# Earlier row writes beside the routing, and a fixed order for a slot's row numbers, in a four-layer mixture-of-experts kernel

## The chip, the cores and the metric

The kernel runs on one core of one Trainium2 chip, as one launch. The metric is the time of an execution on the device in microseconds (us), and the number that counts is the median over several runs. Inside the core, five engines take instructions from queues of their own and work through them in order: TensorE (PE) multiplies matrices, VectorE (DVE) and ScalarE (ACT) do elementwise work, GpSimd (POOL) and SyncE (SP) here mainly issue transfers. [...]

## The reference, cut to what matters

Four layers act on 2048 tokens of 256 channels. Each adds to the tokens the output of an expert network whose input is conditioned first:

```python
x = x + _L0_ffn_ref(_L0_cond_ref(x, cond_1024, ...), ...)
x = x + _L1_ffn_ref(_L1_cond_ref(x, cond_1024, ...), ...)
x = x + _L2_ffn_ref(_L2_cond_ref(x, cond_1024, ...), ...)
x = x + _L3_ffn_ref(_L3_cond_ref(x, cond_1024, ...), ...)
return x
```

Three of these steps have the shape that the change touches: a shared feed-forward network over all tokens, and eight routed experts of which each token uses two. `_L2_cond_ref` and `_L3_cond_ref` are

```python
shared = silu(xf @ w1) * (xf @ w3) @ w2
s = sigmoid(concat([xf, tf]) @ router_W)
_, topk_idx = top_k(s + router_bias, 2)
gates = s_sel / (denom + 1e-09)
h = gelu(einsum('nc,ech->enh', xf, W1e)); y = einsum('enh,ehc->enc', h, W2e)
out = (shared + einsum('ne,enc->nc', combine, y)) / (N_SHARED + 2)
```

and `_L2_ffn_ref` is the same with gated experts of 1024 hidden channels. Layer 2's conditioning has 1024 hidden channels in its shared part, layer 3's has 512. All numbers are 32-bit floats.

## The kernel before

**Tiling.** Tokens lie in SBUF twice: by channel (`XT`, `HT`) as input of matrix products, and by token in 16 tiles of 128 (`Xt`, `Ht`). Routed experts aren't computed densely. Each token's row is written to the DRAM buffer `xbuf` at a place sorted by expert, two places per token. A slot is then 128 such rows, all of one expert; 39 slots hold the 4096 rows with their padding. A slot's outputs go to `tbuf` by token, and the two rows of a token are summed later with their gates.

**The order of a step** (`_cond_moe` from L1493 for layer 2's and layer 3's conditioning, `_layer2_ffn` from L1596 for layer 2's main part; the trace names them l2c, l3c and l2f):

1. The shared part for three of the four token blocks (`_shared`, L1202). For each 128 hidden channels it makes two products `spg` and `spu` (L1215), a silu `ssg` on ACT (L1220), a product `sa` on DVE (L1222) and the second matrix product `spo` (L1225). After each it calls a hook. In l2c and l2f there are 8 such steps in a block, 24 in all; in l3c 4 in a block, 12 in all.
2. Into these steps the class `Lead` (L298) puts the routing. It cuts a generator `routing` in two parts: scores and ranks first, then, in the second part, row numbers, gates and the list of row writes (`lead.sends`, made by `Rows.paced`). `Lead(k, routing, at, per)` runs the parts at the hooks that `at` names: hooks 2 and 4 in l2c and l2f, 1 and 3 in l3c. At each later hook from `late` + 1 on it issues `per` row writes: two in l2c and l2f, four in l3c. There are 32 row writes, one for each of 16 token tiles and two choices.
3. A row write (`Rows.scatter`, L277) is an indirect transfer that POOL issues. When it comes from a hook it carries a real wait on that hook's `sa` product.
4. The slots. `Slots.rows` loads the slot's 128 rows into `xs` (L293, issued by SP; it waits for all 32 row writes), PE turns them (`ps_cm`, L350), DVE copies them to `xsT` (L1369). From two extra columns of `xs` DVE makes each row's target in `tbuf`: `sn` (L1373), 1 for a row that isn't of the slot's expert, and `sdst` (L1375). In the conditioning stages the slot's products are `cph` (L1394) with a gelu `ch` on ACT (L1397), `cpo` (L1400), and a copy `ys` on DVE (L1402). POOL writes `ys` to `tbuf` at `sdst` (L277 again).
5. The fourth token block of the shared part, into whose steps the sums by token are put, and then the next step or, behind l3c, the last expert layer.

**What sets the order.** The program is written as one sequence. A scheduler orders each engine's queue before the launch, by its own estimate of what is ready when; on the chip the order is fixed. `_behind(k, inst, ref)` (L1195) is an order for this scheduler alone: `inst` is put behind `ref` on its engine, with no semaphore. Tiles come from pools with a fixed number of buffers: `xs` has 4, `xsT` 3, `sn` 3, `sdst` 5, `ys` 4. An instruction that writes a tile waits until the readers of the buffer's former content are done; for `sdst` the reader is the row write to `tbuf`, for `xs` they are PE's turn and DVE's `sn` and `sdst`. Weights of a slot's expert (`ring`, L1351) are loaded by SP into four sets in turn.

Of the kernel before, what the change touches and what calls it, by code (L numbers as in the profile page):

```python
# [14 lines left out]
ALU = mybir.AluOpType  # L15
# [5 lines left out]
D = 256  # L21
# [19 lines left out]
class Ring:  # L41


    def __init__(self, t, n):
        self.t, self.n, self.i, self.held = t, n, 0, set()
# [215 lines left out]
class Rows:  # L261
# [12 lines left out]
    def scatter(self, rows, idx, ref=None, **end):  # L274

        k = self.k
        i = k.nc.gpsimd.indirect_dma_start(out=self.ap, out_offset=bass.IndirectOffsetOnAxis(ap=idx, axis=0),  # L277
                                           in_=rows, in_offset=None, **end)
        group = "%s%d" % (self.ap.tensor.name, self.n)
        k.tc.declare_no_dep(i.ins, group=group, reason="rows of their own")  # L280
        k.tc.add_to_no_dep_group(group, i.ins)
        _after(k, i, self.old)
        if ref is not None:
            _after(k, i, [ref.ins.name])
        self.new.append(i.ins.name)

    def paced(self, rows, idxs):

        todo = [(rows[:, t, :], idx[:, t:t + 1]) for t in range(NT) for idx in idxs]
        return [lambda ref=None, a=a: self.scatter(*a, ref) for a in todo]  # L290
# [7 lines left out]
class Lead:  # L298
# [2 lines left out]

    def __init__(self, k, routing, at, per):
        self.k, self.at, self.per = k, at, per
        self.n, self.sends, self.made, self.late = 0, [], None, max(at) + 1 if max(at) else 0
        self.parts = routing(self)
        while 0 in self.at:
            self.part()
# [5 lines left out]
    def hook(self, f, mul, mm):  # L313
        self.n += 1
        if self.n in self.at:
            self.part()
        elif self.n > self.late:
            for _ in range(min(self.per, len(self.sends))):
                self.sends.pop(0)(mul)
# [26 lines left out]
def _channel_major(k, psum, rows):  # L346

    ps = psum.tile([P, 2, P], F32, name="ps_cm", tag="t", bufs=2)
    for c in range(2):
        k.nc.tensor.transpose(ps[:, c, :], rows[:, c * P:(c + 1) * P], k.ident)  # L350
    return ps
# [19 lines left out]
def _layer0(k):  # L371
# [6 lines left out]
    with ExitStack() as ctx:  # L378
# [59 lines left out]
        def shared(tb, hook=None):  # L438
            po = _shared(k, pool, psum, HT, tb, *shw, hook)
            for i in range(2):  # L440
                t = tb * 4 + i * 2
                nc.vector.tensor_tensor(Xt[:, t:t + 2, :], po[i], Xt[:, t:t + 2, :], ALU.add)
# [752 lines left out]
def _behind(k, inst, ref):  # L1195

    k.tc.add_manual_dep(inst.ins, ref.ins.name,
                        mybir.DependencyInfo(mybir.DependencyClass.NoSync,
                                             mybir.DependencyReason.SCHED_ONLY))


def _shared(k, pool, psum, X, tb, W1, W3, W2, nf, hook=None, mid=None):  # L1202

    nc = k.nc
    cols = slice(tb * TB, (tb + 1) * TB)
    po = [psum.tile([P, 2, D], F32, name="spo%d" % i, tag="o", bufs=2) for i in range(2)]
    mul = None
    for f in range(nf):  # L1210
        pg = psum.tile([P, TB], F32, name="spg", tag="mm")
        pu = psum.tile([P, TB], F32, name="spu", tag="mm")
        for ps, W in ((pg, W1), (pu, W3)):
            for c in range(2):
                mm = nc.tensor.matmul(ps, W[:, c, f * P:(f + 1) * P], X[:, c, cols],  # L1215
                                      start=c == 0, stop=c == 1)
        if mid:
            mid(f, mul, mm)
        sg = pool.tile([P, TB], F32, name="ssg", tag="sg")
        nc.scalar.activation(sg, pg, AF.Silu)  # L1220
        a = pool.tile([P, TB], F32, name="sa")
        mul = nc.vector.tensor_mul(a, sg, pu)  # L1222
        for g in range(4):

            mm = nc.tensor.matmul(po[g // 2][:, g % 2, :], a[:, g * P:(g + 1) * P], W2[:, f, :],  # L1225
                                  start=f == 0 and g % 2 == 0, stop=f == nf - 1,
                                  skip_group_check=True)
        if hook:
            hook(f, mul, mm)
    return po  # L1230
# [124 lines left out]
class Slots:  # L1355
# [7 lines left out]
    def rows(self, i):  # L1363

        k, nc, pool = self.k, self.k.nc, self.pool
        xs = pool.tile([P, DR], F32, name="xs", bufs=4)
        k.x.load(xs, k.xbuf[i * P:(i + 1) * P, :])
        xT = pool.tile([P, 2, P], F32, name="xsT", bufs=3)
        nc.vector.tensor_copy(xT, _channel_major(k, self.psum, xs))  # L1369
        if self.of is not None:  # L1370

            n = pool.tile([P, 1], F32, name="sn", bufs=3)
            nc.vector.tensor_tensor(n, xs[:, D + 1:D + 2], self.of[:, i:i + 1], ALU.not_equal)  # L1373
            self.dst[i] = pool.tile([P, 1], U32, name="sdst", bufs=5)
            nc.vector.scalar_tensor_tensor(self.dst[i], xs[:, D:D + 1], -float(self.base), n,  # L1375
                                           ALU.add, ALU.add)
        return xT

    def put(self, i, y):
# [113 lines left out]
def _cond_moe(k, name, wr, bias, W1, W3, W2, nf, hold, R1, R2, gate_mult, final, lead, next=None):  # L1493
# [47 lines left out]
    def shared(tb, hook=None, mid=None, added=lambda: False):  # L1541
        po = _shared(k, pool, psum, XT, tb, W1, W3, W2, nf, hook, mid)
        for i in range(2):
            t = tb * 4 + i * 2
            if added():
                nc.vector.scalar_tensor_tensor(Ht[:, t:t + 2, :], po[i], final, Ht[:, t:t + 2, :],
                                               ALU.mult, ALU.add)
            else:
                nc.scalar.activation(Ht[:, t:t + 2, :], po[i], AF.Copy, scale=final)
# [586 lines left out]
```

## Time and profile before

| what | value |
|---|---|
| median of 3 runs | 1628.64 us (1625.59 to 1629.28) |
| the profiled execution, whole | 1622.8 us |
| its span on the core | 1621.1 us |
| PE busy | 1473.4 us, 91% |
| PE loading weights (beside it) | 1025.4 us, 63% |
| DVE busy | 497.4 us, 31% |
| ACT busy | 313.2 us, 19% |
| POOL busy | 293.0 us, 18% |
| granted PE clock, mean | 0.95 |
| l2c: shared part to the first turned rows, slots | 380 to 523, 523 to 618 us |
| l2f: shared part, slots | 618 to 796, 796 to about 1160 us |
| l3c: shared part, slots | 1250 to 1322, 1330 to 1429 us |

The stages are read off the trace by the names of the tiles. A share of busy time is an average over stages, and PE's busy time comes from modelled ends of matmuls, so the table only says that PE has the least idle time. What a wait costs has to be looked up in its stage. In lines of the timeline the first number is the start in us from the start of the span, the second the time from the start of the first to the end of the last of the merged instructions. The bracket tells how long the engine had been idle and what released it. "SPq" and "POOLq" are the queues that issue transfers.

### The profile page before, as it was taken

The page shows a single profiled execution, that of the slowest core. Times are in us where ns is not written, and L with a number is a line of the kernel's source. Part 1 is how long each engine was busy: PE and PEld are TensorE (multiplying, and loading weights), DVE is VectorE, ACT ScalarE, POOL GpSimd, SP SyncE. Part 2 cuts the span into 40 slices and gives each one's busy share as a digit, 9 for nine tenths or more (in the row PEclk, how much of TensorE's full clock was granted, in tenths as well). Part 3 has the DMA queues.
Part 4 walks back from the last instruction along what each step waited for, and adds up shares of the span by engine and source line. Part 5 has one row for each costly group of instructions (what it writes and reads, how often), then busy time and mean ns, then how long its engine had stood idle before and what let it go on. Part 6 is the DMA issues. An engine that isn't in the chain of part 4 may idle for free. (4 is left out here: it accounts for less than half of the span.)

```text
span 1621.1 us, 23665 instructions
## 1 busy us (share of the span) xinstructions
PE 1473.4 (91%) x8570; PEld 1025.4 (63%) x8570; DVE 497.4 (31%) x1654; ACT 313.2 (19%) x637; POOL 293.0 (18%) x306
## 2 busy tenths in 40 slices
PE   5989998967999999999999999999999978985697
PEld 2543333533555885555699999999975547853575
DVE  3732221323411444421211111111114413448532
ACT  2311211112111112211111111111112111125322
POOL 0400000200132441023100000000000253430242
PEclk9889999967999999999999999999999999995699
DMA  9769994803211574051154055146336347573171
GB/s 248 253 209 341 346 345 147 233 34 117 79 47 53 183 231 136 1 190 51 40 180 169 28 183 179 46 159 225 120 102 228 104 146 233 169 232 110 59 239 36
DMA packets 184241, 252.46 MB, mean 156 GB/s; under 512 B 17111, under 2 KB 137823, under 8 KB 184112
## 3 DMA queue, kind: packets, MB, share of 16 engines
q1 hardware_dynamic: 164448, 210.92, 40.0%
q0 software_dynamic: 14176, 36.63, 6.4%
q10 hardware_dynamic: 5488, 3.25, 0.7%
q8 instruction: 74, 1.21, 0.3%
q14 instruction: 55, 0.45, 0.1%
HBM read 284.86 MB, written 50.76 MB: 207 GB/s over the span
## 5 line engine op out<-in xcount | busy, mean ns | idle before, releaser
L277 POOL DMA_INDIRECT tbuf<-ys,sdst x114 | 112.2, 984 | 522.4 <-ACT ys L1426 217.6
L1225 PE MATMUL spo<-ring,sa 128*128 128x256 f32 x768 | 191.8, 392 | 16.1 <-DVE sa L1222 16.0
L1225 PEld LDWEIGHTS spo<-ring,sa 128*128 128x128 f32 x768 | 140.0, 191 | 98.6 <-DVE sa L1222 78.6
L1222 DVE TENSOR_TENSOR sa<-ssg,spu 128x512 f32<-128x512 f32 x96 | 65.8, 686 | 319.4 <-PE spu L1215 308.5
L1417 PE MATMUL fpg<-xsT,ring 128*128 128x128 f32 x1152 | 141.6, 276 | 5.9 <-ACT ys L1426 5.9
L1417 PEld LDWEIGHTS fpg<-xsT,ring 128*128 128x128 f32 x1152 | 135.8, 192 | 10.4 <-ACT ys L1426 9.4
L1417 PE MATMUL fpu<-xsT,ring 128*128 128x128 f32 x1152 | 140.4, 275 | 0.0
L1417 PEld LDWEIGHTS fpu<-xsT,ring 128*128 128x128 f32 x1152 | 134.4, 192 | 0.0
L1424 PE MATMUL fpo<-ring,fa 128*128 128x256 f32 x576 | 130.7, 380 | 1.8 <-DVE fa L1421 1.8
L1220 ACT ACTIVATE ssg<-spg 128x512 f32<-128x512 f32 x96 | 57.3, 597 | 341.7 <-PE spg L1215 339.2
L1424 PEld LDWEIGHTS fpo<-ring,fa 128*128 128x128 f32 x576 | 106.7, 190 | 15.5 <-DVE fa L1421 2.5
L1215 PE MATMUL spg<-HT,ring 128*128 128x512 f32 x192 | 100.5, 611 | 5.5 <-PEq L474 2.9
L1215 PE MATMUL spg<-XT,ring 128*128 128x512 f32 x192 | 99.0, 605 | 4.7 <-ACT XT L892 4.7
L1421 DVE TENSOR_TENSOR fa<-fsg,fpu 128x512 f32<-128x512 f32 x72 | 49.2, 686 | 149.6 <-PE fpu L1417 149.6
L1400 PE MATMUL cpo<-ring,ch 128*128 128x256 f32 x312 | 88.0, 406 | 5.6 <-ACT ch L1397 4.2
L1215 PE MATMUL spu<-HT,ring 128*128 128x512 f32 x192 | 92.1, 601 | 0.0
L1215 PE MATMUL spu<-XT,ring 128*128 128x512 f32 x192 | 90.5, 594 | 0.0
L1394 PEld LDWEIGHTS cph<-xsT,ring 128*128 128x128 f32 x624 | 84.3, 198 | 9.4 <-DVE xsT L1369 4.3
L1394 PE MATMUL cph<-xsT,ring 128*128 128x128 f32 x624 | 85.5, 282 | 4.0 <-DVE xsT L1369 3.5
L1420 ACT ACTIVATE fsg<-fpg 128x512 f32<-128x512 f32 x72 | 43.0, 597 | 179.6 <-PE fpg L1417 179.6
L1369 DVE COPY xsT<-ps_cm 128x256 f32<-128x256 f32 x138 | 53.2, 419 | 78.0 <-PE ps_cm L350 77.7
L1400 PEld LDWEIGHTS cpo<-ring,ch 128*128 128x128 f32 x312 | 53.9, 192 | 21.1 <-ACT ch L1397 15.2
(550 smaller groups left out, 1608.0 us busy)
## 6 DMA issues: line engine op xcount, KB each, us to landing
ring<-in_L_w SPq DMA_DIRECT2D x108, 1024.0 KB
ring<-in_L_r SPq DMA_DIRECT2D x96, 512.0 KB
ring<-in_L_r SPq DMA_DIRECT2D x156, 256.0 KB
xs<-xbuf SPq DMA_DIRECT2D x138, 129.0 KB
ring<-in_L_W SPq DMA_DIRECT2D x32, 512.0 KB
yt<-tbuf SPq DMA_DIRECT2D x48, 256.0 KB
xbuf<-ACC SPq DMA_DIRECT2D x1, 6063.0 KB
ring<-in_L_s SPq DMA_DIRECT2D x6, 512.0 KB
```

Of the source, the lines that this page charges most:

```text
L277: i = k.nc.gpsimd.indirect_dma_start(out=self.ap, out_offset=bass.IndirectOffsetOnAxis(ap=idx, axis=0), in_=rows, in_offset=None, **end)
L1215: mm = nc.tensor.matmul(ps, W[:, c, f * P:(f + 1) * P], X[:, c, cols], start=c == 0, stop=c == 1)
L1220: nc.scalar.activation(sg, pg, AF.Silu)
L1222: mul = nc.vector.tensor_mul(a, sg, pu)
L1225: mm = nc.tensor.matmul(po[g // 2][:, g % 2, :], a[:, g * P:(g + 1) * P], W2[:, f, :], start=f == 0 and g % 2 == 0, stop=f == nf - 1, skip ...
L1369: nc.vector.tensor_copy(xT, _channel_major(k, self.psum, xs))
L1394: nc.tensor.matmul(ph[:, f, :], R1[:, c, f * P:(f + 1) * P], xT[:, c, :], start=c == 0, stop=c == 1)
L1400: nc.tensor.matmul(po, h[:, f, :], R2[:, f, :], start=f == 0, stop=f == 1)
L1417: nc.tensor.matmul(ps[:, j, :], W[:, c, (f0 + j) * P:(f0 + j + 1) * P], xT[:, c, :], start=c == 0, stop=c == 1)
L1420: nc.scalar.activation(sg, pg, AF.Silu)
L1421: nc.vector.tensor_mul(a[:, f0:f0 + 4, :], sg, pu)
L1424: nc.tensor.matmul(po, a[:, f, :], W2[:, f, :], start=f == 0, stop=f == 4 * nh - 1)
```

## The change

It has two parts. In `Lead`, the first hook that issues row writes is one earlier (`late` loses its + 1), and at the hook that runs the last part of the routing, `per` row writes are issued at once, without the wait on the hook's product. In `Slots.rows`, `sn` and `sdst` are put behind the copy of the slot's turned rows in DVE's order.

```diff
-        self.n, self.sends, self.made, self.late = 0, [], None, max(at) + 1 if max(at) else 0
+        self.n, self.sends, self.made, self.late = 0, [], None, max(at)
...
         self.n += 1
         if self.n in self.at:
             self.part()
+            if not self.at:
+
+                for _ in range(min(self.per, len(self.sends))):
+                    self.sends.pop(0)()
         elif self.n > self.late:
             for _ in range(min(self.per, len(self.sends))):
                 self.sends.pop(0)(mul)
...
-        nc.vector.tensor_copy(xT, _channel_major(k, self.psum, xs))
+        turned = nc.vector.tensor_copy(xT, _channel_major(k, self.psum, xs))
         if self.of is not None:
 
             n = pool.tile([P, 1], F32, name="sn", bufs=3)
-            nc.vector.tensor_tensor(n, xs[:, D + 1:D + 2], self.of[:, i:i + 1], ALU.not_equal)
+            j = nc.vector.tensor_tensor(n, xs[:, D + 1:D + 2], self.of[:, i:i + 1], ALU.not_equal)
+            _behind(k, j, turned)
             self.dst[i] = pool.tile([P, 1], U32, name="sdst", bufs=5)
-            nc.vector.scalar_tensor_tensor(self.dst[i], xs[:, D:D + 1], -float(self.base), n,
-                                           ALU.add, ALU.add)
+            j = nc.vector.scalar_tensor_tensor(self.dst[i], xs[:, D:D + 1], -float(self.base), n,
+                                               ALU.add, ALU.add)
+            _behind(k, j, turned)
         return xT
```

The slots of layer 0 use the same class without `of` and so have neither `sn` nor `sdst`.

## The prediction

> **What bounds the kernel now.** I read the page's shares first. TensorE (PE) is busy 1473.4 us of the 1621.1 us span, VectorE (DVE) 497.4, GpSimd (POOL) 293.0. So an edit to DVE or POOL order pays only where PE stands idle for it. I therefore cut the trace into stages. The diff touches three of them, each a shared feed-forward part followed by routed slots: layer 2's conditioning (l2c), layer 2's main part (l2f), layer 3's conditioning (l3c). In each, 32 row writes (POOL, L277) fill `xbuf`. Only when all have landed may SP load a slot's rows `xs` (L293), which PE turns (`ps_cm`, L350) and DVE copies out (`xsT`, L1369). The timeline of layer 3 where the shared part ends (columns: start, us, engine, line, operation, idle before and its releaser):
>
> ```profile
> 1320.20 1.99 PE L1225 MATMUL spo<-ring,sa 128*128 128x256 f32 x8 [0.85 <-DVE sa L1222]
> ...
> 1324.21 0.96 POOL L277 DMA_INDIRECT xbuf<-Xt,l3c_rows  x1 [0.30 <-issue]
> 1327.47 3.61 SPq L293 DMA_DIRECT2D xs<-xbuf  x6
> 1329.51 0.16 DVE L1373 TENSOR_TENSOR sn<-xs,l3c_of 128x1 f32<-128x1 f32 x1 [9.37 <-DMA xs<-xbuf]
> ...
> 1329.53 1.20 PE L350 MATMUL ps_cm<-ident,xs 128*128 128x128 f32 x4 [7.34 <-DMA xs<-xbuf]
> ...
> 1330.81 3.49 PE L1394 MATMUL cph<-xsT,ring 128*128 128x128 f32 x16
> ```
>
> PE is done at 1320.20 + 1.99 = 1322.19 and idles 7.34 us. The chain behind it is last row write (start 1324.21), 3.26 us until SP may load, 2.04 us until the rows are there. The same place in layer 2 shows no such idle:
>
> ```profile
> 513.76 0.16 DVE L1373 TENSOR_TENSOR sn<-xs,l2c_of 128x1 f32<-128x1 f32 x1 [0.88 <-DMA xs<-xbuf]
> ...
> 522.76 0.60 PE L350 MATMUL ps_cm<-ident,xs 128*128 128x128 f32 x4
> ```
>
> There the rows lie in SBUF 9.0 us before PE turns them (l2f: 786.62 against 795.59, again 9.0 us). The reason is the pace: 24 steps with two writes each in layer 2, only 12 steps with four each in layer 3, so layer 3's last four belong to the very last step.
>
> The second place is the slots. What PE waited for between 1322 and 1425 us (total, times, longest):
>
> ```profile
> PE ps_cm L350 <- DMA xs<-xbuf: 9.2, 2, 7.3
> PE cph L1394 <- DVE xsT L1369: 3.5, 2, 2.1
> PE cpo L1400 <- ACT ch L1397: 1.8, 9, 0.2
> ```
>
> The middle row is what the second edit aims at; the timeline shows its larger case:
>
> ```profile
> 1342.43 0.16 DVE L1375 SCALAR_TENSOR_TENSOR sdst<-xs,sn 128x1 uint32<-128x1 f32 x1 [1.77 <-DMA tbuf<-ys,sdst]
> 1342.51 0.75 DVE L1369 COPY xsT<-ps_cm 128x256 f32<-128x256 f32 x2
> 1342.98 1.27 PE L1394 MATMUL cph<-xsT,ring 128*128 128x128 f32 x9 [2.08 <-DVE xsT L1369]
> ```
>
> The turned rows had been ready since 1339.7, but DVE runs in order, and ahead of the copies stood `sdst`, whose buffer (one of five) was held by an earlier slot's write to `tbuf`.
>
> **Part one, the leads.** The late write step moves from one after the next hook to the routing hook itself: `per` writes go with the routing, `per` with the next hook. Nothing is added or removed; all 32 writes keep their number and their order on POOL. In l3c the row numbers are ready here:
>
> ```profile
> 1274.92 0.15 DVE L250 CAST l3c_rows<-l3c_rows_f 128x16 uint32<-128x16 f32 x1
> ...
> 1275.73 0.69 DVE L1222 TENSOR_TENSOR sa<-ssg,spu 128x512 f32<-128x512 f32 x1
> ...
> 1282.12 0.96 POOL L277 DMA_INDIRECT xbuf<-Xt,l3c_rows  x1 [80.04 <-DVE sa L1222]
> 1283.38 0.96 POOL L277 DMA_INDIRECT xbuf<-Xt,l3c_rows  x1 [0.30 <-issue]
> ```
>
> The first four now start at about 1275.4 (numbers at 1275.07), four more are released by the product at 1276.42. A write costs POOL 1.26 us from start to start (1282.12 to 1283.38), four cost 5.05, a step 5.42 (products at 1281.15 and 1286.57). With four ahead from the start, POOL runs without a gap: last start 1275.4 + 31 x 1.265 = 1314.6 instead of 1324.21. The last release, after the tenth product (1281.15 + 5 x 5.42 + 0.69 = 1308.9), is earlier than POOL comes to it. Landing 1317.9, rows in SBUF 1319.9, before PE's 1322.19. POOL's queue is empty for 80 us before, so nothing is moved past there. On SP the loads stand behind twelve bias loads into `XT` that wait for PE's reads; the last four are issued from 1318.56 to 1320.34. Kept in that order, the rows are there at 1320.34 + 2.04 = 1322.4. Idle left: 0.2 us, **gain 7.1**. If the scheduler turns the first rows inside the shared part, as it does in layer 2, it is 7.3 and up to a microsecond of copying more; if all of it were hidden elsewhere, 0. I take 7.1, the row's value.
>
> In l2c and l2f the writes end two steps (10.8 us) earlier, behind rows that already lie ready 9.0 us early: nothing.
>
> **The clock after a stall**, the granted clock being the column after POOL:
>
> ```profile
> 1330.00:1334.00 4.00, 3.92 (x19) 3.51 (x18) 1.91 (x11) 0.38 (x1) 0.00 (x0) 0.51 0.36 104
> ...
> 1342.00:1348.00 6.00, 5.01 (x25) 4.43 (x25) 1.92 (x7) 0.77 (x2) 1.21 (x2) 0.72 0.58 179
> ```
>
> After the 7.34 us idle PE ran 4 us at 0.51; the sixteen `cph` took 3.49 us against 1.95 for the same sixteen in l2c: 1.5 us. After the 2.08 us idle it ran 6 us at 0.72: 6 x 0.28 = 1.7 us. [...] the row shows that here 2 us are enough. I go by the row: **1.5** for the entry, 1.7 with the next part.
>
> [...] The four early writes now meet the end of the gate arithmetic, 1275.2 to 1277.0. At worst POOL loses these 1.8 us, and the rows still land at 1321.7, before 1322.19. The nearest row says less: writes to `tbuf` beside a DVE busy 42% (38.6 of 92 us, l2c's slots) take 983 ns, those to `xbuf` beside a quiet one 958. Nothing is charged.
>
> **Part two, row numbers behind the turned rows.** A pure order on DVE; the two instructions keep their 0.16 us. In the slots of l3c the copy no longer waits behind a held `sdst`. Gone are 2.08 us with its 1.7 of clock, and the second case, 1.46 us at 1364.19: **5.2**. Late next is `sdst` itself, now behind its copy: a copy leads its slot's `ys` by about 4.0 us (542.22, 546.22), so the `ys` five slots back (2.22 us each) is 7.1 us old by then, and its `tbuf` write needs some 4 to 5 (issued 1337.64, seen 1342.4). Mostly no wait remains; where one does, `ys` queues behind it, with two PSUM buffers of cover. Bounds: 0 and 5.2; I take all, since both cases are this pattern, and book losses separately. In l2f PE is busy 345.9 of 352 us and waits for no copy: 0. In l2c no PE wait names `xsT`: 0.
>
> The cost: `sn` and `sdst` read `xs` too, so the buffer (four) comes free later, by copies (0.75) and the two small ones, about 1 us where the load follows at once. PE waited for `xs` 3.9 us in five places in l2c and once 1.9 us in l3c's slots. I charge 0.5 us for each of these six, **3**, between 0 (SP's order sets the loads anyway) and 1 us for each plus 1.7 of clock for some, 10.
>
> **Sum.** 7.1 + 1.5 + 5.2 - 3 = 10.8 us. A cross-check without these terms: from first `cph` to last `cpo`, l2c's 39 slots take 92.2 us (525.61 to 617.8), l3c's same 39 take 98.3 (1330.81 to 1429.1); 6.1 us can go there, beside 7.1 at the entry: 13.2. What follows, token sums and the last expert layer, waits for these slots and moves along. The profiled execution took 1622.8 us (1621.1 plus 1.7 around); it would become 1612. It lies below all three runs shown, so I subtract from their median: 1628.64 - 10.8 = 1617.8. **Forecast 1617.8**, its own range 1612 to 1623.
>
> **Rivals.** (1) Only the entry moves. `sdst` is held anyway, and the wait goes from the copy to the next copy; the 5.2 fall away: 1628.64 - 8.6 + 3 = 1623.0. For it: DVE is in order, a held `sdst` blocks something in any place. Against it: the ages above. (2) The entry is hidden in vain: slots that start 7 us earlier meet their weights later, as the DMA share is 0.93 from 1348 to 1362 and 283 GB/s from 1375 to 1390. Then 7.1 us come back as waits on `ring`, with the 1.5 of clock behind them; 2.2 remain: 1626.4. Against it: no PE wait names `ring` now. (3) Slower: the loop over the four `xs` buffers decides. In both conditioning stages 27 loads on SP waited last for DVE (13 and 14 by the queue's waits). If each comes 0.8 us later with no slack behind it, that is 21.6 us, against 13.8 gained: 1628.64 + 7.8 = 1636.4. The point: rows landing later than PE's turn in more than every second pair of slots. Against it: in l2c's steady part (540 to 550) loads are issued 2.3 us after their buffer was free. (4) The first writes don't go early, because they take a place behind the next step's: POOL has nothing else queued, so I give this no chance of its own.
>
> Chances: forecast 0.62, rival 1 0.18, rival 2 0.12, rival 3 0.08. About 0.2% (3.3 us) is what a measurement of this kernel can tell from no change. Faster: the forecast and rival 1, 0.80; within: rival 2, 0.12; slower 0.08. The range 1610 to 1628 reaches down to all 13.8 without loss plus a low run, up to rival 2.
>
> **What would show it.** Right: l3c's first row write near 1275 and last near 1315 relative to the same stage; the PE wait for `xs` at the entry under 1 us; no clock near 0.5 behind it; PE's wait for `xsT` in l3c gone. Wrong: more PE waits for `xs` in l2c than 3.9 us, `sdst` waits turning up ahead of `ys` with PE idle at `cpo`, or PE waits on `ring`.

## The result and the profile after

| what | before | after |
|---|---|---|
| median of 13 runs each, side by side | 1624.17 us (1617.48 to 1631.36) | 1612.52 us (1607.96 to 1616.79) |
| ratio, with its 95% interval | | 0.9919 (0.9903 to 0.9934) |
| profiled execution, span | 1621.1 us | 1611.1 us |
| PE busy | 1473.4 us | 1466.1 us |
| DVE busy | 497.4 us | 491.7 us |
| granted PE clock, mean | 0.95 | 0.953 |

By the medians the change makes the kernel 11.7 us faster (1624.17 - 1612.52, 0.72%). The ratio, here and below, is worked out apart from the medians and says 0.81%, 13.2 us. The forecast difference was 10.8 us, and that fits. The forecast time, 1617.8 us, lies 5.3 us too high: it started from a median of three runs, 1628.64, and that of thirteen is 4.5 us lower. Whether the parts of the forecast fit has to be looked up in the stages. The timeline of after where layer 3's shared part ends answers to the first extract of the prediction (line numbers behind the edits stand four to six further down than before):

```profile
1320.75 0.96 POOL L277 DMA_INDIRECT xbuf<-Xt,l3c_rows  x1 [0.30 <-issue]
...
1323.65 1.75 SPq L293 DMA_DIRECT2D xs<-xbuf  x4
...
1326.42 1.77 SPq L1857 DMA_DIRECT2D XT<-in_L_b  x4
1327.04 0.60 PE L354 MATMUL ps_cm<-ident,xs 128*128 128x128 f32 x4
...
1328.06 1.99 PE L1229 MATMUL spo<-ring,sa 128*128 128x256 f32 x8 [0.41 <-DVE sa L1226]
1328.25 0.15 DVE L1377 TENSOR_TENSOR sn<-xs,l3c_of 128x1 f32<-128x1 f32 x1
...
1329.89 1.95 PE L1400 MATMUL cph<-xsT,ring 128*128 128x128 f32 x16
```

The last row write (first line) now starts 7.3 us before the last `spo` (1328.06), where before it started 4.0 us after it. The first rows are turned inside the shared part, at 1327.04, and the sixteen `cph` follow the last `spo` without an idle time and in 1.95 us. The last write is 6 us later than the forecast's 1314.6, because several groups of four had to wait for the product of a step that came late (more on these steps below). The clock in the first 4 us of the slots, 0.51 before, and over the slots, 0.94 before (the column after POOL's):

```profile
1330.00:1334.00 4.00, 3.66 (x29) 3.32 (x28) 1.14 (x7) 2.54 (x4) 0.00 (x0) 1.00 0.64 180
...
1330.00:1422.00 92.00, 85.81 (x546) 74.83 (x545) 37.47 (x150) 16.75 (x41) 37.41 (x38) 1.00 0.66 209
```

The three largest rows of what PE waited for from 1321 to 1422 us (the row of `cph` on `xsT` is gone, and that of `ps_cm` on `xs` has shrunk from 9.2 us to 1.2; the 1.7 us before one `ps_cm` are new, and the profile shows no cause for them):

```profile
PE cpo L1406 <- ACT ch L1403: 2.0, 8, 0.3
PE ps_cm L354 <- issue: 1.7, 1, 1.7
PE ps_cm L354 <- DMA xs<-xbuf: 1.2, 2, 0.8
```

The same for DVE's wait that stood ahead of the copies, in before (1322 to 1431) and in after (1322 to 1425):

```profile
DVE sdst L1375 <- DMA tbuf<-ys,sdst: 13.6, 9, 3.2
```

```profile
DVE sdst L1380 <- DMA tbuf<-ys,sdst: 0.6, 1, 0.6
```

And the first row writes of layer 3's conditioning, from POOL's timeline of after:

```profile
1274.58 1.13 POOL L277 DMA_INDIRECT xbuf<-Xt,l3c_rows  x1 [70.24 <-DVE l3c_rows_w L246]
1276.01 0.96 POOL L277 DMA_INDIRECT xbuf<-Xt,l3c_rows  x1 [0.30 <-issue]
```

They start with the row numbers, no longer with a step's product `sa`, as the prediction read the change.

Cut into stages by the names of the tiles, the two executions and those of the experiments below compare like this (us; each from one profile, read to about 0.2 us). "l2c, l3c shared" run from the stage's first routing scores to its first `cph` (l2c) or to the end of its last `spo` before the slots (l3c), "entry" from there to the first `cph`, "slots" to the next stage's scores (l2c), to the end of the last `fpo` (l2f) or to the start of the last `cpo` (l3c):

| kernel | up to l2c | l2c shared | l2c slots | l2f slots | l3c shared | l3c entry | l3c slots |
|---|---|---|---|---|---|---|---|
| before | 405.2 | 120.4 | 152.7 | 402.0 | 61.7 | 8.5 | 97.9 |
| e5, before again | 402.9 | 120.5 | 153.1 | 408.1 | 63.7 | 8.3 | 95.7 |
| after | 408.5 | 120.4 | 154.6 | 399.1 | 69.4 | -0.3 | 91.6 |
| e4, after again | 405.2 | 120.5 | 154.4 | 399.1 | 72.3 | -0.3 | 91.0 |
| e1, leads alone | 404.4 | 120.4 | 154.0 | 406.5 | 73.5 | -0.3 | 97.1 |
| e2, order alone | 405.3 | 120.4 | 153.7 | 399.1 | 65.7 | 8.2 | 94.5 |
| e3, `sdst` deep | 401.9 | 120.5 | 152.9 | 400.4 | 64.5 | 8.7 | 91.0 |
| e9, order and `xs` deep | 403.2 | 120.4 | 151.0 | 399.1 | 61.4 | 8.4 | 88.8 |
| e12, after and `xs` deep | 407.9 | 120.5 | 151.1 | 399.1 | 61.4 | -0.3 | 87.6 |

The first column is a stretch that neither part touches, and it varies between 401.9 and 408.5. So spans of single profiles can't be compared to a few us. Stages can with more care: the two profiles of before show how far one kernel's own stages differ, most in l2f's slots (402.0 and 408.1).

From before to after the entry gives 8.8 us, l3c's slots 6.3, l2f's slots 2.9; l2c's slots cost 1.9 and l3c's shared part 7.7. Two of these were not in the prediction: l2f's slots and l3c's shared part. Two stretches that are not in the table were shorter in after too, the one between l2f's slots and l3c's scores (60.1 to 58.1) and all behind l3c's slots (192.0 to 189.3); over the profiles of all the kernels here they vary by 2.0 and 3.1 us, so nothing is concluded from them.

### The profile page after: what moved, and what is told of

The parts are those of the page before. It is cut to its first block, busy times and chain, and to the rows that moved or that the text cites. A ratio compares the mean times of both kernels' runs of the same rounds, so it can differ in the third digit from the quotient of the medians.

```text
span 1611.1 us, 23661 instructions
## 1 busy us (share of the span) xinstructions
PE 1466.1 (91%) x8570; PEld 1021.6 (63%) x8570; DVE 491.7 (31%) x1654; ACT 313.1 (19%) x637; POOL 293.5 (18%) x306
## 5 line engine op out<-in xcount | busy, mean ns | idle before, releaser
L1373 DVE COPY xsT<-ps_cm 128x256 f32<-128x256 f32 x138 | 56.8, 421 | 84.0 <-PE ps_cm L354 77.8
L1406 PEld LDWEIGHTS cpo<-ring,ch 128*128 128x128 f32 x312 | 53.1, 189 | 19.5 <-ACT ch L1403 12.9
```

What stands on the lines that cost most here:

```text
L1373: turned = nc.vector.tensor_copy(xT, _channel_major(k, self.psum, xs))
L1406: nc.tensor.matmul(po, h[:, f, :], R2[:, f, :], start=f == 0, stop=f == 1)
```

## The experiments

**e1, the leads alone.** The change without the three hunks in `Slots.rows`.

```diff
-        self.n, self.sends, self.made, self.late = 0, [], None, max(at) + 1 if max(at) else 0
+        self.n, self.sends, self.made, self.late = 0, [], None, max(at)
...
+            if not self.at:
+
+                for _ in range(min(self.per, len(self.sends))):
+                    self.sends.pop(0)()
```

> The lead part alone. Prediction's theory: 8.6 us faster than before (7.1 of entry, 1.5 of clock), ratio near 0.9947; PE's wait for xs at the entry of layer 3's slots falls from 7.3 us to under 1, the first sixteen cph take about 1.95 us instead of 3.49, and PE's waits for xsT in those slots (3.5 us before) stay, because sdst may still be ahead of the copies. Rival A (the lead is all of it): the whole 0.9919, about 13 us. Rival B (the writes that now run earlier disturb the shared part of layer 3, where the trace of after has two PE stalls of 3.5 and 2.3 us): 3 us or less, and the same two stalls stand in this trace too.

Median 1619.76 us, ratio 0.9973 (0.996 to 0.9986): between the theory and rival B, and rival B's stalls are there. The profiled execution was the slowest of its 18 (1627.18 us), so its stages can be longer than usual. **e2, the order alone**, is the change without these hunks of `Lead`.

```diff
+            _behind(k, j, turned)
...
+            _behind(k, j, turned)
```

> The order of sn and sdst alone. Prediction's theory: 2.2 us faster (5.2 gained in layer 3's slots, 3 lost because xs buffers come free later), ratio near 0.9986; the entry stall of 7.3 us stays, no PE wait for xsT in layer 3's slots. A second reading, from the trace of after: layer 2's main part gains too, because there fa stood behind a held sdst (1.8 us of PE waits before, none after); then 4 to 7 us, ratio 0.996 to 0.9975. Rival C (the loop over the xs buffers decides): slower, above 1.001.

Median 1615.52 us, ratio 0.9949 (0.9929 to 0.9969). The forecast gave the leads 8.6 us and the order 2.2 after its losses; against the same runs of before (median 1624.59) they gave 4.8 and 9.1. The division was wrong both ways. The second reading of e2 named the right place, and even its 4 to 7 us were too few.

Where the order's surplus comes from is seen in l2f. DVE's and PE's waits there, before (796 to 1250 us):

```profile
DVE sdst L1375 <- DMA tbuf<-ys,sdst: 118.7, 20, 9.9
...
PE fpo L1424 <- DVE fa L1421: 1.8, 3, 0.9
```

The upper row looks harmless, since DVE has time. But DVE is in order: behind a held `sdst` stands not only the slot's copy, but `fa`, the product that the next `fpo` needs. One of four such places in e1's timeline:

```profile
951.33 0.60 ACT L1424 ACTIVATE fsg<-fpg 128x512 f32<-128x512 f32 x1 [2.98 <-PE fpg L1421]
...
954.18 0.16 DVE L1379 SCALAR_TENSOR_TENSOR sdst<-xs,sn 128x1 uint32<-128x1 f32 x1 [10.91 <-DMA tbuf<-ys,sdst]
954.29 1.28 DVE L1425 TENSOR_TENSOR fa<-fsg,fpu 128x512 f32<-128x512 f32 x2
955.03 5.41 PE L1428 MATMUL fpo<-ring,fa 128*128 128x256 f32 x16 [1.96 <-DVE fa L1425]
```

`fsg` is there at 951.93, `sdst` at 954.18 only, `fa` behind it, and PE idles 1.96 us. The sixteen `fpo` then take 5.41 us instead of 3.72, at a granted clock of 0.71:

```profile
955.03:961.00 5.97, 5.84 (x20) 4.63 (x20) 0.85 (x2) 0.37 (x1) 0.00 (x0) 0.71 0.55 221
```

With the order, the whole answer on PE's waits from the end of l2f's shared part to 1150 us, near the end of its slots, has no `fpo` any more (e2):

```profile
PE fpg L1419 <- ACT ys L1428: 5.2, 15, 0.3
PE spo L1225 <- DVE sa L1222: 0.4, 1, 0.4
```

l2f's slots took 402.0, 408.1 and 406.5 us in the three profiles without the order and with five `sdst`, and 399.1 in every one with the order.

**e3, more buffers in place of the order**: before, with twelve `sdst` instead of five, so that none is held. No other line changes.

```diff
-            self.dst[i] = pool.tile([P, 1], U32, name="sdst", bufs=5)
+            self.dst[i] = pool.tile([P, 1], U32, name="sdst", bufs=12)
```

> The kernel before with twelve sdst buffers in place of five, and neither part of the change: DVE is never held by a tbuf write, the order of PE, ACT, POOL and SP stays as before. Theory (the second part pays because a held sdst blocks DVE): 5 to 7 us faster, ratio 0.9957 to 0.997, and no DVE wait of sdst for a tbuf write. Rival D (the second part pays through another schedule on SP and PE, not through the held sdst): no change, 0.999 to 1.001.

Median 1615.97 us, ratio 0.9952 (0.9935 to 0.9969), the order's own within the interval. l2f's slots took 400.4 us and l3c's slots 91.0 (in the fastest of the eight executions, 1609.85 us). So what the order part removes is, for the most part, the held buffer at the head of DVE's queue; to remove the hold in another way brings as much within the interval. It doesn't remove everything in l2f: one `fpo` still waited 1.0 us for `fa`, now behind an `sn` whose rows had not landed.

**e4 and e5** are after and before unchanged, once each beside the runs above and below, for their profiles.

> The changed kernel once more, for its trace alone. Theory: the stalls of 3.5 and 2.3 us in layer 3's shared part are chance of one execution and are gone; from l3c's scores (the copy l3c_s) to the last spo of the shared part it takes 61.6 us as before, not 69.2, and the span is 3 to 7 us shorter than 1611. Rival B: they come from the earlier writes and stand at the same place again.

> The kernel before once more, for its trace alone. Question: is the shared part of layer 3's conditioning, 61.7 us in the first trace of before (from the copy l3c_s to the end of its last spo), usual without the lead? The two traces without the lead that followed have 65.7 and 64.5, the three with it 69.4, 72.3 and 73.5. Theory: 61 to 66 us, with at most one stall of 2.3 to 2.7 us before an spo; the step from there to 69 and more belongs to the lead. Rival (chance of the execution): 69 or more can turn up here too.

They took 1612.94 and 1623.03 us. e4 shows the long shared part of l3c again (72.3 us), against its theory; e5 has a shared part of 63.7 us, as its theory had it, and a longer l2f (408.1 us, with six waits of `fpo` for `fa`, 7.1 us).

**e6, the weights of l3c's first slots later.** In all profiles with the leads so far, l3c's shared part is 4 to 12 us longer than in those without. PE waits there for `sa`, and the engines behind it, DVE and ACT, wait for something that the profile calls "remote". The first theory was that the early row writes meet the 2 MB of slot weights, which are loaded at the same time. e6 is after with these loads behind the eighth step's product:

```diff
-        nc.sync.dma_start(t, a[bass.ds(e, 1)].rearrange("o (c p) f -> p (o c) f", p=P), **new)
+        d = nc.sync.dma_start(t, a[bass.ds(e, 1)].rearrange("o (c p) f -> p (o c) f", p=P), **new)
+        if ref is not None and i < ns:
+            _after(k, d, [ref.ins.name])
```

> The changed kernel, with the first eight weight loads of layer 3's slots (2 MB, issued by SP from about 1275 us on) made to wait for the product of the eighth step of the shared part, some 20 us later. Theory (the early row writes meet these loads on the DMA engines, at a share of 0.9 to 1.06 for 10 us, and what the engines stall for in that time is held up by it): the 5 us stall of the sixth step goes, the shared part of layer 3 takes 62 to 67 us, and the kernel is 3 to 6 us faster than the changed one, ratio 0.988 to 0.990. Rival (the stalls come from the row writes alone, or from the program's length): shared part 69 or more, ratio 0.991 to 0.993.

Median 1611.29 us, ratio 0.9912 (0.9882 to 0.9943); the shared part took 69.8 us, with a wait of 4.8 us for `sa`. The loads moved, the stalls stayed: that theory fell.

**e7, the leads with twelve `sdst`**, without the order.

> The lead and twelve sdst buffers, without the fixed order. Theory (the lead alone gained only half of its entry because it also makes held sdst writes worse in layer 2's main part, 466.6 us against 462.2; what frees DVE takes that away): ratio 0.991 to 0.9925, the same as the change, layer 2's main part at 457 to 459 us. Rival (the two parts simply add and the lead's loss in layer 2 has another cause): layer 2's main part stays above 461 us and the ratio is 0.9935 or more.

Median 1614.42 us, ratio 0.9928 (0.9899 to 0.9957), not told apart from after. The shared part took 70.3 us: the stalls don't hang on the order. The question of the expectation stays undecided, as the ratio lies between its theory's and its rival's. l2f's slots took 402.5 us instead of the 399.1 with the order, and three `fpo` waited 2.4 us in all. No `sdst` is held there; at the head of DVE's queue stands an `sn` that waits for its rows, as in e3:

```profile
1077.47 0.16 DVE L1377 TENSOR_TENSOR sn<-xs,l2f_of 128x1 f32<-128x1 f32 x1 [3.95 <-DMA xs<-xbuf]
...
1078.08 0.69 DVE L1425 TENSOR_TENSOR fa<-fsg,fpu 128x512 f32<-128x512 f32 x1
1078.82 1.99 PE L1428 MATMUL fpo<-ring,fa 128*128 128x256 f32 x8 [0.79 <-DVE fa L1425]
```

The order takes `sn` away from there too, more buffers don't.

**e8, six `xs` buffers** instead of four in the slots of the three stages, for the cost that the prediction charged to the order. (A tile of the last layer that shares these buffers gets the same number.)

```diff
-        xs = pool.tile([P, DR], F32, name="xs", bufs=4)
+        xs = pool.tile([P, DR], F32, name="xs", bufs=4 if self.of is None else 6)
...
-                    w = pool.tile([P, TB], BF16, name="l3f_b", tag="xs", bufs=4)
+                    w = pool.tile([P, TB], BF16, name="l3f_b", tag="xs", bufs=6)
```

> The changed kernel with six xs buffers in place of four in the three stages. Prediction's third cost (row buffers come free later, so rows land later): PE's wait for xs in layer 2's conditioning, 6.0 us in the trace of after against 3.9 before, falls under 2; 3 to 5 us faster than the changed kernel, ratio 0.989 to 0.990. Rival (SP's order, not the buffers, makes rows late): the wait stays at 4 to 6 us, ratio 0.991 to 0.993.

Median 1607.83 us, ratio 0.9884 (0.9855 to 0.9912). PE's wait for rows in l2c's slots, in after and in e8:

```profile
PE ps_cm L354 <- DMA xs<-xbuf: 6.0, 6, 1.7
```

```profile
PE ps_cm L354 <- issue: 1.8, 2, 1.7
PE ps_cm L354 <- DMA xs<-xbuf: 1.7, 2, 1.5
```

l2c's slots fall from 154.6 to 151.3 us, l3c's from 91.6 to 88.6. So the loop over the `xs` buffers, the prediction's rival for "slower", does cost time, in before as well (152.7), though too little to turn the sign.

**e9, order and six `xs` without the leads**, asks what the leads are worth.

> The order part with six xs buffers, without the leads. If the leads keep the 0.27% that they measured alone, this kernel takes about 0.9884 + 0.0027 = 0.991 of the kernel before, 4 us more than the changed kernel with six xs buffers; layer 3's conditioning has its entry stall of 8.2 us again, a shared part of 64 to 66 us, and layer 2's conditioning slots take 150 to 151 us. Rival: what the leads give at the entry is lost again in the shared part, so that with the slots freed of both other waits they are worth nothing: a ratio of 0.988 to 0.989.

Median 1601.53 us, ratio 0.9892 (0.9865 to 0.9919). Against e8 (0.9884) this reads as if the leads were worth next to nothing; but l3c's shared part took 61.4 us here and 70.8 in e8, and e12 below takes this up. **e10, three row writes per step in l3c, and e11, four per step in layer 2**, ask whether row writes without a gap make the stalls.

```diff
-    lead_ = Lead(k, routing, *((2, 4), 2) if nf == 8 else ((1, 3), 4))
+    lead_ = Lead(k, routing, *((2, 4), 2) if nf == 8 else ((1, 3), 3))
```

> The changed kernel with three row writes per step in layer 3's conditioning instead of four: the first three with the routing, POOL busy with them 3.8 of 5.4 us of a step instead of without a gap. Density theory (the stalls inside the shared part come from row writes that follow one another without a gap): no wait for sa above 2.5 us, shared part 64 to 67 us instead of 69 to 73, and the row numbers' last writes come later, so 2 to 5 us of entry stall return. Place theory (the stalls come from where in the program the first writes begin, whatever their pace): shared part stays 69 to 73 us with a wait for sa of 3 to 5 us. Total by both within 4 us of the changed kernel.

```diff
-    lead_ = Lead(k, routing, *((2, 4), 2) if nf == 8 else ((1, 3), 4))
+    lead_ = Lead(k, routing, *((2, 4), 4) if nf == 8 else ((1, 3), 4))
...
-    lead = Lead(k, routing, (2, 4), 2)
+    lead = Lead(k, routing, (2, 4), 4)
```

> The changed kernel with four row writes per step instead of two in both routed steps of layer 2, so that POOL writes without a gap there too, for seven steps from the routing on. Density theory: stalls of DVE's sa or ACT's ssg of 3 to 8 us turn up in layer 2's shared parts, 123 to 130 us instead of 120.4 and 120.1; total 5 to 15 us above the changed kernel. Place theory: both shared parts stay within 0.5 us of 120.4 and 120.1, and the total within 2 us of the changed kernel.

e10: median 1611.17 us, ratio 0.9953 (0.9939 to 0.9967). e11: 1604.80 us, 0.9906 (0.9874 to 0.9938). In all three of this set l3c's shared part took 61.4 us. For e10 that would speak for the density theory, though in its trace the first fourteen writes of l3c still follow one another at 1.27 us and only the later ones leave gaps. But e11 has after's row writes in l3c, without a gap, and takes 61.4 us too; that speaks against it, and so do l2f's shared part, 120.1 us with writes without a gap, and l2c's, 126.0 us: longer, but for a reason that has a name. In e11's timeline:

```profile
461.69 0.18 DVE L1287 TENSOR_SCALAR Xt<-tok 128x16 f32<-128x16 f32 x1 [8.50 <-DMA xbuf<-Xt,l2c_rows]
461.79 0.69 DVE L1226 TENSOR_TENSOR sa<-ssg,spu 128x512 f32<-128x512 f32 x1
```

An instruction that changes `Xt` may not run before the row writes have read it, and in this order it stood ahead of `sa`. e10 is a measure of the entry instead. With the writes thinned, the rows came late again, at the slots' entry:

```profile
1315.49 0.96 POOL L277 DMA_INDIRECT xbuf<-Xt,l3c_rows  x1 [0.30 <-issue]
1318.87 4.68 SPq L293 DMA_DIRECT2D xs<-xbuf  x6
...
1320.86 1.30 PE L354 MATMUL ps_cm<-ident,xs 128*128 128x128 f32 x4 [6.12 <-DMA xs<-xbuf]
```

The entry took 7.2 us (2 to 5 were expected), and the ratio, 0.9953, is that of the order alone, 0.9949, though from another set. This fits leads that pay through the entry alone.

**e12, the program of e8 once more**, to tell the writes from the occasion.

> The changed kernel with six xs buffers once more, the program of e8 unchanged. In e9, e10 and e11, which shared one chip, layer 3's conditioning had no stall for an unseen cause in its shared part (61.4 us), though e11 has the same early row writes there as the changed kernel; in e8, on another chip, the shared part took 70.8 us. Chip theory (these stalls belong to the chip or the execution, not to the writes): if it runs on that chip again, the shared part takes 61 to 62 us and the total is some 8 us under e9's 1601.5, a ratio of 0.983 to 0.985; on another chip it varies. Write theory (early row writes cause them): 69 to 73 us wherever it runs, ratio 0.988 to 0.989.

Median 1598.86 us (1592.6 to 1600.5), ratio 0.9847 (0.9823 to 0.9871), on a chip recorded under the same number as e8's. The same place in layer 3's shared part, in e8:

```profile
1284.87 0.69 DVE L1226 TENSOR_TENSOR sa<-ssg,spu 128x512 f32<-128x512 f32 x1 [7.56 <-remote]
...
1285.61 1.99 PE L1229 MATMUL spo<-ring,sa 128*128 128x256 f32 x8 [2.82 <-DVE sa L1226]
...
1292.61 0.60 ACT L1224 ACTIVATE ssg<-spg 128x512 f32<-128x512 f32 x1 [11.76 <-remote]
...
1293.98 2.43 PE L1229 MATMUL spo<-ring,sa 128*128 128x256 f32 x5 [2.94 <-DVE sa L1226]
```

and in e12:

```profile
1284.13 1.99 PE L1229 MATMUL spo<-ring,sa 128*128 128x256 f32 x8
...
1289.55 1.99 PE L1229 MATMUL spo<-ring,sa 128*128 128x256 f32 x8
...
1294.97 1.99 PE L1229 MATMUL spo<-ring,sa 128*128 128x256 f32 x8
```

(The extract of e8 ends at 1296 us, within the last row's eight `spo`.) One program, 70.8 us there and 61.4 here. So early row writes without a gap are not enough to make these stalls, and the chip's number doesn't decide either; by the expectation's own numbers the write theory fell. The ratio is where the other put it, 0.983 to 0.985. In us e12 lies only 2.7 under e9 and not 8, as before took 2.7 us more in this set too (1621.03 against 1618.36). e12 is also the best version that was run: 22.2 us below before (1621.03 in the same set).

## Why the prediction held, and where its parts were off

**Entry gain, 7.1 us, and its clock, 1.5 us: right.** The entry falls from 8.5 us to -0.3 (PE turns the first rows inside the shared part, the prediction's own alternative), the first sixteen `cph` from 3.49 us to 1.95. The row numbers were ready when the prediction had it, and in e12, without stalls, the last write starts 53.1 us after l3c's scores, where the forecast's 1314.6 is 54.0 after them. Without stalls in the shared part the leads keep the gain: e12's ratio lies 0.0045 under e9's, 7.3 us at 1621, and in the stages the entry differs by 8.7 us and the slots by 1.2. (The two ran in different sets, and their intervals touch.) SP's order was not as the prediction argued: the first four `xs` loads went ahead of the last four bias loads, 1323.65 against 1326.42.

**No loss charged in l3c's shared part: wrong on these occasions.** In e1, 4.8 us were left of 8.6. The stage shows where they can have gone: the shared part takes 69.4 to 73.5 us in after, e1, e4, e6, e7 and e8, 61.7 to 65.7 in before, e2, e3 and e5. By e12 the writes alone don't make these stalls. In the executions that had any, those with the leads had the larger ones: the longest stall of PE ahead of a `spo` was 2.6 us in e2, 2.3 in e3, 1.9 in e5, and 2.9 to 5.0 in after, e1, e4, e6, e7 and e8. It goes by occasion: in each of the first three (the two first profiles; e1 to e4; e5 to e8) all shared parts with the leads are longer than those without, and in the last two (e9 to e11; e12) all take 61.4 us, with the leads or not. This fits early writes that lengthen a stall of another origin, but it is not shown, and chance over a few profiles is not ruled out. What DVE and ACT wait for is open too.

**Order in l2f, 0 us: wrong.** This is the term that was mis-sized most: 2.9 us from before to after, and 7.4 and 9.0 from e1 and e5 to the 399.1 us of the ordered kernels. The step that failed is the sentence "in l2f PE is busy 345.9 of 352 us and waits for no copy". The copy was indeed not waited for. But the row "PE fpo <- DVE fa: 1.8, 3" stood in the trace, and the 118.7 us of DVE's wait above it said what held `fa`. In e5, the same program, the `fpo` waits came to 7.1 us.

**Order in l3c's slots, 5.2 us: right in kind.** The waits for `xsT` are gone with the order (e2) or with more buffers (e3). From e1 to after the slots fall by 5.5 us; from before to e2 by 3.4, and from e5, before's second profile, by 1.2. In e2 PE waits more for rows behind the entry, 4.0 us against 1.9 in before. The 1.7 us of clock in this term were one row's: behind a longer wait, 2.82 us in e8, the clock stayed at 1.00 (last section). So the size is known to a few us only. Rival 1, that a held `sdst` blocks something in any place, falls: 13.6 us of DVE's waits for `tbuf` became 0.6.

**The `xs` buffers' loss, 3 us: right in kind.** l2c's slots cost 1.9 us more after than before (1.0 in e2), against 2.5 charged for five waits of 0.5. e8 shows that it comes from the buffers. One of the prediction's signs of being wrong, more than 3.9 us of waits for `xs` in l2c, turned up here (6.0 us), but only to the size of the charge.

**Leads in layer 2, 0 us: right.** Its shared part takes the same in every profile with two writes per step (120.4 and 120.5 in the table for l2c). Behind it l2c's slots are 1.3 us longer in e1 than in before; with before's own two profiles 0.4 apart, this is small, but not the zero of the forecast. Rival 2, waits on `ring`, has no row in after's answer, of which three rows stand above.

So 10.8 us came out nearly right by luck, because two errors went against each other: by the medians the leads fell 3.8 us short of their term (the longer stalls in l3c's shared part can account for this), and the order brought 6.9 us more than its own (l2f's slots above all). By the two parts measured alone, 0.9973 and 0.9949 multiply to 0.9922, after's 0.9919: within their intervals the parts add up.

## What to carry to other kernels

On an engine that works in order, as DVE did here (`fa` behind the held `sdst` at 954.18 in e1), ask of every instruction that waits for a buffer what stands behind it, in all stages and not only where the copy next to it is late; a small wait of the bound engine for that engine, together with a large one of that engine for a transfer, is the sign. More buffers removed the hold here (e3, ratio 0.9952); the order took the waiting instruction out of the way also where it waited for rows (no wait of `fpo` for `fa` in e2, 1.0 us in e3), and the buffer that is then freed later wants a look too (l2c's waits for `xs`, 6.0 us in after, 1.7 in e8). And where a change shifts work inside a stage, compare stages over several profiles of the same kernel, taken on more than one occasion, before a difference of a few us is put down to the change.

## What the runs showed of the hardware

- Two executions of one program differed by 9.4 us in a stage of some 60 us (e8, 70.8; e12, 61.4) through stalls of DVE and ACT that the profile puts down to no engine or transfer of the kernel.
- An idle time of PE of 1.96 us was followed by a granted clock of 0.71 over the next 6 us (e1), one of 2.08 us by 0.72 (before). The prediction read from before's row that 2 us are enough. That reading went too far. Elsewhere in before the clock stayed at 1.00 over the 6 us behind an idle time of 1.94 us (at 611.43), and in one trace, e8, it stayed up behind 2.82 us (first row) and fell behind 2.94 (second row):

```profile
1285.60:1293.90 8.30, 5.43 (x16) 2.96 (x16) 0.66 (x1) 0.60 (x1) 3.84 (x4) 1.00 0.20 72
1293.98:1300.00 6.02, 6.02 (x14) 3.94 (x15) 0.00 (x0) 0.60 (x1) 3.84 (x4) 0.72 0.24 88
```

  So a wait of about 2 us can cost clock here, but in these traces its length alone doesn't say whether it will.
- The first of the early row writes, beside DVE's gate arithmetic, took 1.13 us instead of 0.96 in after, the second 0.96 again; e12 shows the same two times. The 1.8 us that the prediction set as the worst case for POOL here, and did not charge, was its author's estimate. No more than 0.17 us shows, and that the arithmetic is the cause of it is not shown.
